# Graph layer in fp32 on one core: s added to x from PSUM tile by tile, three relus of four on ScalarE, no memsets on GpSimd, 104 early tiles instead of 96

## The chip, the cores and the metric

The kernel runs on one core of one Trainium2 chip. The metric is the device time of one execution in microseconds. Times shown as "runs" are medians of repeated executions; the profile is one further execution. The engines are named as in the profile: PE (TensorE) with PEld for its weight loads, DVE (VectorE), ACT (ScalarE), POOL (GpSimd) and SP (SyncE, which issues transfers only).

## The reference: what is computed

There are 12500 nodes with 160 features each (64 scalars and 32 vectors of 3) and 400000 edges, sorted by their target. Cut to what matters here:

```python
h = jnp.maximum(_layernorm(x, axis=-1), 0.0)       # no weight, no bias
s = [h0 @ W_sc0, h1 @ W_sc1] * a                   # per node, a = node_vec1
y = [h0 @ W_l1_0, h1 @ W_l1_1] * a                 # per node
w = silu(edge_attr_16 @ fc_W1) @ fc_W2             # per edge, 192 wide
mid = products of w, y[src] and edge_attr_4        # per edge, 96 scalars and 96 vectors
z = zeros.at[dst].add(mid)                         # sums over the edges of a node
out = x + C_S * s + C_X * [z0 @ W_l2_0, z1 @ W_l2_1] * a
```

The constant scales are folded into the weights in the kernel.

## The kernel before, in words

**Node stage.** The 98 tiles of 128 nodes are worked in 49 steps of two tiles; four steps are a group of eight tiles. `acc` in SBUF holds all of x, and later the output. The steps run as a software pipeline written out by hand: for each q the loop calls the stages with their lags, so that `turn_rows` of step q - 2 stands beside `center` of step q. `center` (DVE) takes mean and variance of each tile (`bn_stats`, `bn_aggr`) and makes h, the relu of x minus the mean: for the first tile of the step on DVE, for the second on ACT (`center_second`, with the negated mean `less` as bias). The division by the deviation comes last, since relu lets a positive factor through: `scales` turns the root that ACT took once a group into `ra`, a over the deviation. `turn_rows` (PE) transposes h, `out_of_psum` (ACT) brings it to SBUF as hT, `map_rows` (PE) multiplies with both weights at once, so that a tile of PSUM, `po`, holds y and s side by side, 2 x 160. There are six such banks. `leave` (ACT) scales po by ra into `ys` (y and s, 320 wide), and after the group's last step ACT stores the y half to `y_d` in DRAM. `add_s` (DVE) then adds the s half of the whole group, 8 x 160, to `acc` in one instruction. There are two `ys` buffers.

**Early batches.** The 3125 edge tiles form 782 batches of four. GpSimd gathers what a batch needs by one indirect transfer for each tile: rows of `y_d` by the edges' sources. That can't begin before all of `y_d` is written. So that GpSimd isn't idle in the node stage, it gathers rows of x itself, by the same indices, for some batches that come up later: `gather_x` brings them to `xr`, `keep_x` stores them to a scratch tensor `xr_d` (with a column of zeros set by DVE), and in the edge stage `made_load` ... `made_leave` compute y from them in small pieces between the other batches (statistics, relu, transposes, products with the weights; the node's a by a one-hot product). `made_at` lists these batches: RB of them, RS apart, in a first part (17, every 24 batches) and in a second (7, every 42). `plan` spreads the pieces over the batches before. A call `gather_x(j)` covers two tiles; it waits for hT of step j - 8, so that the gathers keep in step with the node tiles.

**Edge stage.** For each batch: `load` (POOL, four gathers of y into one of 11 buffers; the load of batch b waits for the weights of batch b - 8), `hidden` and `weigh` (PE, ACT: the edge weights in PSUM), `lift_rows` (ACT, L530), `dots_of` and `products` (DVE), `sums` (PE, L690: one-hot selection times products, summed in PSUM over a group of tiles). A finished group is transposed and mapped by PE and added to `acc` by DVE (`accumulate`, L735). The order on PE, ACT, DVE and POOL is that of the program in this stage; in the node stage POOL's and SP's order is made by the scheduler.

Before the edge stage, DVE finds each group's first node from `dst_i` (`first_nodes`, `all_nodes`, `relate`).

Of the kernel before, what the change touches and what calls it, by code (L numbers as in the profile page):

```python
# [17 lines left out]
P = 128  # L18
# [17 lines left out]
WIDE = 3, 5  # L36
GN = 8
HN = 2
RB = 17, 7
RS = 24, 42  # L40
LO = D - P
EPS = 1e-5
C_S = math.sin(math.pi / 8.0)
# [4 lines left out]
def kernel(  # L48
# [286 lines left out]
    engines = {mybir.EngineType.PE, mybir.EngineType.Activation, mybir.EngineType.DVE}  # L335
    with (
        tc.tile_pool(name="nr", bufs=1) as nrp,
        tc.tile_pool(name="nrx", bufs=10) as nrx,
        tc.tile_pool(name="ny", bufs=2) as ny,
        tc.tile_pool(name="ns", bufs=3) as ns,  # L340
        tc.tile_pool(name="nh", bufs=4) as nh,
        tc.tile_pool(name="nd", bufs=3) as nd,
# [30 lines left out]
        def gather_x(j):  # L373

            r, h = divmod(j, 2)
            if h == 0:
                xrs[r] = nrx.tile([P, GT * D + 1], F32, name="xr")
                nc.gpsimd.memset(xrs[r][:, :GT * D], 0.0)
                nc.gpsimd.memset(xrs[r][:, :D], 0.0)
            for k in (2 * h, 2 * h + 1):  # L380
                c = made_at[r] * GT + k
                of = src_first[:, r, k:k + 1] if r < FIRST else src_sb[:, c:c + 1]
                ins = nc.gpsimd.indirect_dma_start(  # L383
                    out=xrs[r][:, k * D:(k + 1) * D], out_offset=None, in_=x,
                    in_offset=bass.IndirectOffsetOnAxis(ap=of, axis=0))
# [10 lines left out]
        def center(q):  # L396

            g, n, j, m = steps[q]
            xt = acc[:, g:g + n, :]
            if j == 0:  # L400
                mvs[g] = ns.tile([P, GN, 2], F32, name="mv")
            mv = mvs[g]
            h = nh.tile([P, HN, D], F32, name="h")
            for k in range(m):
                st = ns.tile([P, 6], F32, name="st")
                nc.vector.bn_stats(st, xt[:, j + k, :])
                nc.vector.bn_aggr(mv[:, j + k, :], st)
                if k == 0:
                    nc.vector.tensor_scalar(h[:, k, :], xt[:, j + k, :], mv[:, j + k, 0:1], 0.0, ALU.subtract, ALU.max)
                else:  # L410
                    less = ns.tile([P, 1], F32, name="less")
                    nc.vector.tensor_scalar(less, mv[:, j + k, 0:1], -1.0, None, ALU.mult)
                    lesses[q] = less
            hs[q] = h
            if j + m == n:
                ra = ns.tile([P, GN], F32, name="ra")
                nc.scalar.activation(ra[:, :n], mv[:, :n, 1], AF.Sqrt, bias=eps)
                ras[g] = ra

        def center_second(q):  # L420

            g, n, j, m = steps[q]
            if m > 1:
                nc.scalar.activation(hs[q][:, 1, :], acc[:, g + j + 1, :], AF.Relu, bias=lesses.pop(q))

        def scales(q):

# [29 lines left out]
        def leave(q):  # L457

            g, n, j, m = steps[q]
            if j == 0:  # L460
                yss[g] = ny.tile([P, GN, 2, D], F32, name="ys")
            ys, ra = yss[g], ras[g]
            for k, po in enumerate(poss.pop(q)):
                nc.scalar.activation(ys[:, j + k, :, :], po, AF.Copy, scale=ra[:, j + k:j + k + 1])
            if j + m == n:
                node_dma(g, n, lambda rows, t, p: nc.scalar.dma_start(by_tile(y_d[rows, :]), ys[:p, t, 0, :]))

        def add_s(q):

            g, n, j, m = steps[q]  # L470
            if j + m == n:
                nc.vector.tensor_add(acc[:, g:g + n, :], acc[:, g:g + n, :], yss[g][:, :n, 1, :])


        with tc.manual_schedule(engines=engines):
# [35 lines left out]
            while begun[0] < 2 * nr:  # L511
                gather_x(begun[0])
                begun[0] += 1
            while kept[0] in xrs:
                keep_x(kept[0])
                kept[0] += 1
            first_nodes()
            edge_weights()
# [42 lines left out]
    with (  # L561
# [486 lines left out]
```

## Time and profile before

| | before |
|---|---|
| runs | median 3971.47 us of 3 (3970.27 to 3972.49) |
| the profiled execution's own time | 3969.84 us |
| its span, first to last instruction | 3967.8 us |
| TensorE's granted clock, mean | 0.976 |
| busy: PE, DVE, ACT, POOL | 92%, 88%, 48%, 76% |
| first gather of y | 150.5 us |
| gathers of y, of x | 3029, 96 |

A row of a timeline is start, duration, engine, line, operation, output and inputs, shape, how many instructions, and in brackets the idle time before it and what ended it. A row of a group is line, engine, operation, shape and count, then busy us and mean ns of one, then idle us before them and what ended it. POOL isn't counted busy in the pause of 0.3 us after each gather, which is why an engine that never waits shows 76%.

### The profile page before, as it was taken

Reading aid. Unit: us, or ns where it says so; the run is one execution under the profiler, and the core shown is the slowest. Engines: PE = TensorE matmul, PEld = TensorE weight load, DVE = VectorE, ACT = ScalarE, POOL = GpSimd, SP = SyncE. Lnnn points to the kernel's source line nnn. Section 1 sums busy time; section 2 is a strip of 40 time slices with the busy share of each in tenths; the row PEclk is TensorE's granted clock in tenths of the full one; section 3 lists DMA queues with packets and bytes.
Section 4 is the critical chain, followed back from the end, with each engine's and each line's share of the span. In section 5 each row is a group of like instructions: output and inputs, shape, how many; then the busy total and the mean of one; then the engine's idle time right before and its main releaser. Section 6 shows DMA issues by size and latency. Waiting matters only on the chain. (4 is left out here: it accounts for less than half of the span.)

```text
span 3967.8 us, 49385 instructions
## 1 busy us (share of the span) xinstructions
PE 3639.7 (92%) x15821; PEld 2102.0 (53%) x15821; DVE 3476.1 (88%) x6732; ACT 1906.6 (48%) x5350; POOL 2997.6 (76%) x3180
## 2 busy tenths in 40 slices
PE   6689999999999999999999989999999899999998
PEld 5445555555555555555555545555555555555554
DVE  6788888998888989989899888888889898989887
ACT  5544444444444444444544444444444444444443
POOL 8777777777777777777777777777777777777775
PEclk9899999999999999999999999999999999999999
DMA  8432333333223332322333332323333232342223
GB/s 267 140 76 74 77 77 79 79 77 79 73 77 77 80 79 77 79 74 77 77 79 79 77 76 74 78 74 76 77 76 77 74 79 74 80 124 76 73 75 84
DMA packets 228574, 334.77 MB, mean 84 GB/s; under 512 B 55098, under 2 KB 171910, under 8 KB 228054
## 3 DMA queue, kind: packets, MB, share of 16 engines
q0 software_dynamic: 150000, 256.20, 26.2%
q1 hardware_dynamic: 64642, 67.02, 5.4%
q10 hardware_dynamic: 13668, 8.36, 0.7%
q8 instruction: 125, 2.05, 0.2%
q14 instruction: 139, 1.14, 0.1%
HBM read 307.49 MB, written 23.88 MB: 84 GB/s over the span
## 5 line engine op out<-in xcount | busy, mean ns | idle before, releaser
L599 POOL DMA_INDIRECT yg<-y_d,src_sb x3029 | 2873.3, 949 | 923.3 <-issue 909.3
L690 PE MATMUL pz<-pr,sel 128*128 128x384 f32 x6250 | 2281.3, 509 | 2.2 <-ACT za L708 2.1
L530 ACT ACTIVATE yge<-yg,raw 128x160 f32<-128x160 f32 x3029 | 1253.7, 426 | 1903.1 <-DMA yg<-y_d,src_sb 1894.5
L690 PEld LDWEIGHTS pz<-pr,sel 128*128 128x128 f32 x6250 | 1150.9, 194 | 831.4 <-issue 227.9
L635 PE MATMUL pw<-w,hT 64*128 64x192 f32 x6250 | 732.1, 353 | 247.9 <-DVE pr L546 235.5
L635 PEld LDWEIGHTS pw<-w,hT 64*128 64x128 f32 x6250 | 497.5, 188 | 639.1 <-DVE pr L546 432.2
L542 DVE TENSOR_TENSOR pr<-pr,pw 128x768 f32<-128x768 f32 (+1 forms) x782 | 745.0, 953 | 27.0
L535 DVE TENSOR_TENSOR tmp<-yg,pw 128x384 f32<-128x384 f32 (+1 forms) x758 | 415.0, 548 | 325.4 <-ACT pw L637 322.5
L537 DVE TENSOR_REDUCE yg<-tmp 128x128 f32<-128x384 f32 (+1 forms) x758 | 449.8, 593 | 27.2 <-ACT yge L530 1.1
L669 DVE TENSOR_TENSOR sel<-pw,drel 128x1536 f32<-128x1536 f32 (+1 forms) x261 | 455.1, 1744 | 0.0
L617 PE MATMUL px<-xe,w 32*128 32x512 f32 x782 | 439.0, 644 | 10.7 <-ACT os L722 4.2
L541 DVE TENSOR_TENSOR pr<-pw,yg 128x384 f32<-128x384 f32 (+1 forms) x758 | 419.7, 554 | 17.8
L546 DVE TENSOR_TENSOR pr<-pw,yge 128x384 f32<-128x384 f32 (+1 forms) x782 | 427.1, 546 | 0.0
L545 DVE TENSOR_TENSOR pr<-pw,yge 128x256 f32<-128x256 f32 (+1 forms) x782 | 325.2, 416 | 0.0
L622 ACT ACTIVATE hT<-px 128x512 f32<-128x512 f32 x391 | 227.1, 581 | 11.7 <-PE px L617 11.5
L617 PEld LDWEIGHTS px<-xe,w 32*128 32x128 f32 x782 | 114.5, 183 | 197.2 <-issue 78.9
L637 ACT ACTIVATE pw<-raw 128x12 f32<-128x12 f32 (+1 forms) x782 | 129.1, 165 | 79.1 <-PE pw L635 78.8
L717 PEld LDWEIGHTS px<-wc,za 128*128 128x128 f32 x720 | 98.1, 191 | 29.2 <-ACT za L708 0.9
L383 POOL DMA_INDIRECT xr<-in_x,src_sb x88 | 93.4, 1061 | 22.7 <-issue 18.1
L735 DVE SCALAR_TENSOR_TENSOR acc<-os,by,acc 128x160 f32 x240 | 92.4, 385 | 18.4 <-ACT os L722 1.4
L717 PE MATMUL px<-wc,za 128*128 128x96 f32 x720 | 96.6, 270 | 0.6 <-ACT za L708 0.6
L704 PEld LDWEIGHTS pz<-ident,zs 128*128 128x128 f32 x360 | 46.7, 141 | 38.1 <-issue 21.1
(128 smaller groups left out, 1567.9 us busy)
## 6 DMA issues: line engine op xcount, KB each, us to landing
yg<-y_d,src_sb POOLq DMA_INDIRECT x3029
xe<-in_e SPq DMA_DIRECT2D x196, 128.0 KB
xr_d<-xr SPq DMA_DIRECT2D x24, 320.5 KB
y_d<-ys ACTq DMA_DIRECT2D x12, 640.0 KB
xm<-xr_d SPq DMA_DIRECT2D x24, 320.0 KB
acc<-in_x SPq DMA_DIRECT2D x11, 640.0 KB
out<-acc SPq DMA_DIRECT2D x11, 640.0 KB
raw<-in_e SPq DMA_DIRECT2D x32, 192.0 KB
```

What stands on the lines that cost most here:

```text
L530: return [nc.scalar.activation(yge[:, k, :], yg[:, k, :], AF.Copy, scale=e4v[:, k, 0:1]).ins for k in range(n)]
L535: return [nc.vector.tensor_tensor(tmp[:, :n], y1, wt[:, :n, NW:NW + 3].unsqueeze(3).to_broadcast([P, n, 3, M1]), ALU.mult).ins, nc.vector. ...
L537: nc.vector.tensor_reduce(yg[:, :n, M0:96], tmp[:, :n].rearrange("p t c u -> p t u c"), AX.X, ALU.add).ins]
L541: return [nc.vector.tensor_mul(pr[:, :n, 0:96], wt[:, :n, 96:NW], yg[:, :n, 0:96]).ins, nc.vector.tensor_mul(pr[:, :n, 256:].rearrange("p ...
L542: nc.vector.tensor_mul(pr[:, :n, 256:].rearrange("p t (c u) -> p t c u", c=3), pr[:, :n, 0:M0].unsqueeze(2).to_broadcast([P, n, 3, M0]), w ...
L545: nc.vector.tensor_mul(pr[:, :n, 96:160], wt[:, :n, 0:M0], yge[:, :n, 0:M0]).ins,
L546: nc.vector.tensor_mul(pr[:, :n, 160:256].rearrange("p t (c u) -> p t c u", c=3), wt[:, :n, M0:96].unsqueeze(2).to_broadcast([P, n, 3, M1] ...
L599: ins = [nc.gpsimd.indirect_dma_start(out=yg[:, k, :], out_offset=None, in_=y_d, in_offset=bass.IndirectOffsetOnAxis(ap=src_sb[:, t:t + 1] ...
L617: nc.tensor.matmul(ph, w1[r, :], xe[r, :], start=True, stop=True)
L635: ins.append(nc.tensor.matmul(pw[:, k, 0:NW], hids[s][r, o:o + P], w2[r, :], start=True, stop=True).ins)
L669: ins = nc.vector.tensor_tensor(sels[u][:, 0:n, :].rearrange("p t (k c) -> p t k c", k=GT), for_each, drel[:, u * TG:u * TG + n].unsqueeze ...
L690: nc.tensor.matmul(z_ps[g], sels[t // TG][:, t % TG, :], pr[:, k, M0:], start=first, stop=last)
```

## The change

It does six things.

- `add_s` runs for each step with lag 5: for each tile one `scalar_tensor_tensor` that reads the s half of `po` from PSUM, multiplies by ra and adds to `acc`. The addition of 8 x 160 a group goes.
- `leave` evacuates only the y half, 160 wide, and `ys` is half as large, with three buffers instead of two.
- In odd steps both relus run on ACT, in even steps one as before: three of four. `less` has two columns.
- The two memsets of each `xr` on GpSimd go. Its buffers are 13 instead of 10.
- There are 9 early batches in the second part, 33 apart, instead of 7, 42 apart: 104 early tiles instead of 96. Their pieces are 6 batches apart with lag 2, as in the first part, instead of 12 with lag 6.
- `scales` has lag 2 instead of 1; the load of dst is issued at step 24 instead of at the start; the `keep_x` calls left after the loop follow `first_nodes` and `edge_weights`.

```diff
-RB = 17, 7
-RS = 24, 42
+RB = 17, 9
+RS = 24, 33
...
-        tc.tile_pool(name="nrx", bufs=10) as nrx,
-        tc.tile_pool(name="ny", bufs=2) as ny,
+        tc.tile_pool(name="nrx", bufs=13) as nrx,
+        tc.tile_pool(name="ny", bufs=3) as ny,
...
                 xrs[r] = nrx.tile([P, GT * D + 1], F32, name="xr")
-                nc.gpsimd.memset(xrs[r][:, :GT * D], 0.0)
-                nc.gpsimd.memset(xrs[r][:, :D], 0.0)
...
+            of = range(m) if q % 2 else range(1, m)
             for k in range(m):
...
-                if k == 0:
+                if k not in of:
                     nc.vector.tensor_scalar(h[:, k, :], xt[:, j + k, :], mv[:, j + k, 0:1], 0.0, ALU.subtract, ALU.max)
-                else:
-                    less = ns.tile([P, 1], F32, name="less")
-                    nc.vector.tensor_scalar(less, mv[:, j + k, 0:1], -1.0, None, ALU.mult)
-                    lesses[q] = less
+            if len(of):
+                less = ns.tile([P, HN], F32, name="less")
+                nc.vector.tensor_scalar(less[:, of[0]:m], mv[:, j + of[0]:j + m, 0], -1.0, None, ALU.mult)
+                lesses[q] = of, less
...
-            if m > 1:
-                nc.scalar.activation(hs[q][:, 1, :], acc[:, g + j + 1, :], AF.Relu, bias=lesses.pop(q))
+            if q in lesses:
+                of, less = lesses.pop(q)
+                for k in of:
+                    nc.scalar.activation(hs[q][:, k, :], acc[:, g + j + k, :], AF.Relu, bias=less[:, k:k + 1])
...
-                nc.scalar.activation(ys[:, j + k, :, :], po, AF.Copy, scale=ra[:, j + k:j + k + 1])
+                nc.scalar.activation(ys[:, j + k, :], po[:, 0, :], AF.Copy, scale=ra[:, j + k:j + k + 1])
...
-            if j + m == n:
-                nc.vector.tensor_add(acc[:, g:g + n, :], acc[:, g:g + n, :], yss[g][:, :n, 1, :])
+            for k, po in enumerate(poss[q]):
+                to = acc[:, g + j + k, :]
+                nc.vector.scalar_tensor_tensor(to, po[:, 1, :], ras[g][:, j + k:j + k + 1], to, op0=ALU.mult, op1=ALU.add)
...
-            nc.sync.dma_start(dst_i, dst)
...
+                if q == min(24, last):
+                    nc.sync.dma_start(dst_i, dst)
...
-                for stage, lag in ((scales, 1), (center_second, 1), (out_of_psum, 3), (leave, 6), (turn_rows, 2), (map_rows, 4),
-                                   (center, 0), (add_s, 7)):
+                for stage, lag in ((scales, 2), (center_second, 1), (out_of_psum, 3), (leave, 6), (turn_rows, 2), (map_rows, 4),
+                                   (center, 0), (add_s, 5)):
...
-            step, lag = (6, 2) if b * GT <= wide else (12, 6)
+            step, lag = 6, 2
```

What this makes of the instructions' order, at three places. On GpSimd, at the very start (x of the first batches; the numbers tell buffers apart, and a name in brackets is the semaphore's owner that is waited for: DMAHW for SP's and ACT's transfers, DMASW for GpSimd's own). Before:

```order
L378 MEMSET xr_194 128x640
L378 MEMSET xr_201 128x640
L379 MEMSET xr_194 128x160 [waits Pool_49]
L379 MEMSET xr_201 128x160 [waits Pool_49]
L378 MEMSET xr_208 128x640
L383 DMA xr_194<-in_x,src_first_141 128x160 [waits DMAHW0_49,Pool_49]
L383 DMA xr_194<-in_x,src_first_141 128x160 x3
```

And now, after the same memset of `wor`:

```order
L490 MEMSET wor_107 128x480
L381 DMA xr_193<-in_x,src_first_141 128x160 [waits DMAHW0_49]
L381 DMA xr_193<-in_x,src_first_141 128x160 x3
L381 DMA xr_198<-in_x,src_first_141 128x160 [waits DMAHW2_49]
L381 DMA xr_198<-in_x,src_first_141 128x160 x3
L381 DMA xr_203<-in_x,src_sb_69 128x160 [waits DMAHW6_49,DMASW0_49]
```

Of the memsets none is left; the first gather waits for the transfer of its indices alone.

On DVE, around the end of a group's statistics in the node stage. Before, two tiles of one step and the addition of the group two before:

```order
L406 BN_STATS st_462<-acc_111 128x6
L407 BN_AGGR mv_403<-st_462 128x2 [waits DVE_49]
L409 TENSOR_SCALAR h_461<-acc_111,mv_403 128x160 [waits DVE_49,PE_49]
L406 BN_STATS st_466<-acc_111 128x6
L407 BN_AGGR mv_403<-st_466 128x2 [waits DVE_49]
L412 TENSOR_SCALAR less_469<-mv_403 128x1 [waits DVE_49,Activation_49]
L472 TENSOR_TENSOR acc_111<-acc_111,ys_333 128x1280 [waits Activation_49]
```

And now, one odd step, without a relu on DVE:

```order
L405 BN_STATS st_485<-acc_111 128x6
L406 BN_AGGR mv_394<-st_485 128x2 [waits DVE_49]
L405 BN_STATS st_488<-acc_111 128x6
L406 BN_AGGR mv_394<-st_488 128x2 [waits DVE_49]
L411 TENSOR_SCALAR less_491<-mv_394 128x2 [waits DVE_49,Activation_49]
L474 SCALAR_TENSOR_TENSOR acc_111<-po0_135,ra_374,acc_111 128x160 [waits PE_49,Activation_49]
L474 SCALAR_TENSOR_TENSOR acc_111<-po1_136,ra_374,acc_111 128x160 [waits PE_49,Activation_49]
```

Every step now ends on DVE with two additions that wait for PE, and for ACT's earlier reading of the bank.

On ACT, the evacuations of one step and the store of a group. Before:

```order
L424 ACTIVATE h_640<-acc_111,less_648 128x160 [waits DMAHW1_49,DVE_49]
L445 ACTIVATE hT_656<-pt0_133 128x512 [waits PE_49,Activation_49]
L464 ACTIVATE ys_568<-po4_139,ra_500 128x320
L464 ACTIVATE ys_568<-po5_140,ra_500 128x320
L466 DMA y_d_60<-ys_568 128x8x160 [waits DMAHW7_49,Activation_49]
```

And now:

```order
L425 ACTIVATE h_637<-acc_111,less_645 128x160 [waits DMAHW1_49,DVE_49]
L446 ACTIVATE hT_655<-pt0_133 128x512 [waits PE_49,Activation_49]
L465 ACTIVATE ys_566<-po4_139,ra_493 128x160 [waits DVE_49]
L465 ACTIVATE ys_566<-po5_140,ra_493 128x160 [waits DVE_49]
L467 DMA y_d_60<-ys_566 128x8x160 [waits DMAHW3_49,Activation_49]
```

The evacuations now wait for DVE, which reads s from the same bank first; the store still waits for an earlier transfer on a semaphore that it shares with SP's.

More of the change, by code (lines that the diff above doesn't have):

```diff
@@ L460, in leave @@
             if j == 0:
-                yss[g] = ny.tile([P, GN, 2, D], F32, name="ys")
+                yss[g] = ny.tile([P, GN, D], F32, name="ys")
             ys, ra = yss[g], ras[g]
             for k, po in enumerate(poss.pop(q)):
-                nc.scalar.activation(ys[:, j + k, :, :], po, AF.Copy, scale=ra[:, j + k:j + k + 1])
+                nc.scalar.activation(ys[:, j + k, :], po[:, 0, :], AF.Copy, scale=ra[:, j + k:j + k + 1])
             if j + m == n:
-                node_dma(g, n, lambda rows, t, p: nc.scalar.dma_start(by_tile(y_d[rows, :]), ys[:p, t, 0, :]))
+                node_dma(g, n, lambda rows, t, p: nc.scalar.dma_start(by_tile(y_d[rows, :]), ys[:p, t, :]))
         def add_s(q):
             g, n, j, m = steps[q]
-            if j + m == n:
-                nc.vector.tensor_add(acc[:, g:g + n, :], acc[:, g:g + n, :], yss[g][:, :n, 1, :])
+            for k, po in enumerate(poss[q]):
+                to = acc[:, g + j + k, :]
+                nc.vector.scalar_tensor_tensor(to, po[:, 1, :], ras[g][:, j + k:j + k + 1], to, op0=ALU.mult, op1=ALU.add)
         with tc.manual_schedule(engines=engines):
@@ L513 @@
                 begun[0] += 1
+            first_nodes()
+            edge_weights()
             while kept[0] in xrs:
@@ L516 @@
                 kept[0] += 1
-            first_nodes()
-            edge_weights()
     before.close()
```

## The prediction

> **What bounds the kernel now.** I read the page first, then the waits of the whole span, then GpSimd's own timeline, because the shares alone mislead: TensorE is busy 92% and GpSimd only 76%.
>
> ```profile
> span 3967.8 us, 49385 instructions
> ## 1 busy us (share of the span) xinstructions
> PE 3639.7 (92%) x15821; PEld 2102.0 (53%) x15821; DVE 3476.1 (88%) x6732; ACT 1906.6 (48%) x5350; POOL 2997.6 (76%) x3180
> ```
>
> Among the groups on the page are the gathers of y, and those of x (busy us, mean ns of one, idle before):
>
> ```profile
> L599 POOL DMA_INDIRECT yg<-y_d,src_sb x3029 | 2873.3, 949 | 923.3 <-issue 909.3
> ```
>
> ```profile
> L383 POOL DMA_INDIRECT xr<-in_x,src_sb x88 | 93.4, 1061 | 22.7 <-issue 18.1
> ```
>
> The second view is the table of waits over the whole span (engine and line, what it waited for, total us, times, longest).
>
> ```profile
> ACT yge L530 <- DMA yg<-y_d,src_sb: 1894.5, 2209, 3.9
> POOL yg L599 <- issue: 909.3, 2983, 0.3
> ```
>
> The gathers of y wait for nothing but their own issue, never longer than 0.3 us, while ScalarE waits 2209 times for what they fetch. GpSimd is the bound of the whole edge stage, with idle time only between its own instructions. Its timeline gives the rate and the places of the start and the end:
>
> ```profile
> 3.79 1.09 POOL L383 DMA_INDIRECT xr<-in_x,src_first  x1 [0.17 <-POOL xr L378]
> ...
> 74.33 1.60 POOL L383 DMA_INDIRECT xr<-in_x,src_sb  x1 [0.30 <-issue]
> ...
> 149.23 0.97 POOL L383 DMA_INDIRECT xr<-in_x,src_sb  x1 [0.30 <-issue]
> 150.51 0.95 POOL L599 DMA_INDIRECT yg<-y_d,src_sb  x1 [0.30 <-issue]
> ...
> 3945.87 0.94 POOL L599 DMA_INDIRECT yg<-y_d,src_sb  x1 [0.30 <-issue]
> ```
>
> From the first gather of y to the last, the 3029th, are 3795.4 us, 3028 steps of 1.2534 us. After the last one 21.9 us remain to the end of the span; they are the last products and the stores, which the change doesn't touch. So the span is: when the first gather of y starts (150.5), plus 1.2534 us for each gather of y, plus 21.9 us. The change can act on the first two only.
>
> What sets 150.5? GpSimd came straight from its last gather of x (149.23). It wasn't waiting for y, which was ready earlier. ScalarE's timeline shows this:
>
> ```profile
> 18.48 0.58 ACT L445 ACTIVATE hT<-pt 128x512 f32<-128x512 f32 x1
> ...
> 131.03 0.61 ACT L445 ACTIVATE hT<-pt 128x512 f32<-128x512 f32 x1
> ...
> 139.51 1.28 ACT L622 ACT_TABLE_LOAD   x1 [3.90 <-DMA y_d<-ys]
> ```
>
> The first and last rows of hT are those of steps 0 and 48 of the node stage: 112.55 us for 48 steps, 2.345 us each. The table load waited for the last stores of y, so y was complete at 139.5, which is 8.5 us after the last hT and 11.0 us before GpSimd came for it. **In the node stage, too, GpSimd was last.**
>
> **The change, part by part.** Fewer gathers of y: 26 batches instead of 24 are made early, so 104 tiles of x are gathered instead of 96, and 3021 of y instead of 3029. In the edge stage that is 8 x 1.2534 = 10.0 us less. The 8 gathers of x go ahead of it, where they cost the same if GpSimd is last there, and nothing if it would wait for y anyway.
>
> GpSimd ahead of the first gather of y. Its 146.7 us from 3.79 to 150.51 hold 96 gathers (120.3 us at 1.2534), the memsets, and something else. These are groups of lines in the first 165 us, shapes apart:
>
> ```profile
> L472 DVE TENSOR_TENSOR acc<-acc,ys 128x1280 f32<-128x1280 f32 x12 | 17.8, 1487 | 4.6 <-ACT ys L464 4.6
> ...
> L378 POOL MEMSET xr<- 128x640 f32 x24 | 17.1, 725 | 0.0
> ...
> L379 POOL MEMSET xr<- 128x160 f32 x24 | 5.7, 244 | 0.4
> ```
>
> The memsets sum to 22.8 us. Five stand ahead of the first gather, at most 2.7 us by these means (3 x 0.725 + 2 x 0.244), and some lie within the pause that a gather has anyway. The rest of the 26.4 us is in the gathers themselves: those of x take 1061 ns, those of y 949, which makes 88 x 0.112 = 9.9 us, and the long ones stand under VectorE's large additions, as the 1.60 us at 74.33 does under the one at 73.63:
>
> ```profile
> 13.51 2.54 DVE L409 TENSOR_SCALAR h<-acc,mv 128x160 f32<-128x160 f32 x1
> ...
> 23.53 0.30 DVE L409 TENSOR_SCALAR h<-acc,mv 128x160 f32<-128x160 f32 x1
> 23.75 0.32 DVE L406 BATCH_NORM_STATS2 st<-acc 128x6 f32<-128x160 f32 x1
> ...
> 73.63 1.48 DVE L472 TENSOR_TENSOR acc<-acc,ys 128x1280 f32<-128x1280 f32 x1
> ...
> 3957.50 0.81 DVE L735 SCALAR_TENSOR_TENSOR acc<-os,by,acc 128x160 f32 x2 [0.83 <-ACT os L722]
> ```
>
> Both go: the memsets by the edit, the large additions because s now comes from PSUM tile by tile. For that form the nearest row is L735, which runs 240 times between gathers of 949 ns, so I take no hold-up from it. GpSimd would be through with x at 3.8 + 104 x 1.2534 = 134.2; at best 2.7 earlier (no memsets ahead of the first gather), and some 2 us later where VectorE's cast of dst falls on gathers as the additions did: 131.5 to 136.
>
> A rule of the Trainium skill speaks to this (SBUF — State Buffer, Who interferes with whom): an addition with both inputs in SBUF contends with GpSimd's reads only, and building descriptors needs the write interface, an inference by its own words. By that the additions hold up no gather and the 9.9 us would stay; the stretched gathers disagree, and I go by them (what would follow otherwise is the fourth rival).
>
> The node stage itself, which now may come last. VectorE per step of two tiles: the large addition goes (1.487 / 4 = 0.37 us), and so does half a relu, which held VectorE for 23.75 - 23.53 = 0.22 us (0.11 a step). Two additions from PSUM come. No row has that form at this size: at most it costs what L735 does, 0.81 us for two; at least what the relu does, 0.44. I take 0.75, near L735, which is the same operation. VectorE changes by -0.04 to +0.33 us a step, my value +0.27. ScalarE gains half a relu a step, 24 in all, and evacuates half the width 98 times; these are its groups in the same window:
>
> ```profile
> L464 ACT ACTIVATE ys<-po,ra 128x320 f32<-128x320 f32 x98 | 46.3, 535 | 5.2 <-DMA y_d<-ys 4.7 <-ACT ys L464 0.5
> ```
>
> ```profile
> L424 ACT ACTIVATE h<-acc,less 128x160 f32<-128x160 f32 x49 | 21.0, 429 | 30.9 <-DVE less L412 15.8 <-DVE mv L407 6.7 <-DVE st L406 3.9
> ```
>
> Half as wide, an evacuation costs between half of 535 and the 429 of a relu of that width; with 24 x 429 ns added that is -16 to 0 us, and 30.9 us of idle time before the relus is left. ScalarE doesn't set the pace.
>
> Waits that fall:
>
> ```profile
> DVE ra L431 <- ACT ra L417: 12.9, 9, 6.0
> ```
>
> ```profile
> ACT ys L464 <- DMA y_d<-ys: 4.7, 3, 3.0
> ```
>
> With the scales a step later (lag 2) VectorE no longer stands at the reciprocal right behind ScalarE's root, and with three y buffers ScalarE needn't wait for the store two groups back. Together they are 17.6 us, 0.37 a step. Not all goes: ScalarE's stores still wait in turn with SP's transfers, and VectorE now waits for TensorE's results at every step. I take 0.2 of it. The pace is then 2.345 + 0.27 - 0.2 = 2.4 us, between 1.95 and 2.68. Step 0 comes earlier by the relu at 13.51, which took 2.54 us under GpSimd's memsets instead of 0.30: 18.5 - 2.2 = 16.2. So y is complete at 16.2 + 48 x 2.4 + 8.5 = 139.9.
>
> **What is late next** is thus the node stage, not GpSimd: GpSimd would be free at 134 and wait some 6 us for y. Only here does it stop being the bound. The sum: the first gather of y starts at 139.9 instead of 150.5, -10.6; 8 gathers less, -10.0; together -20.6 us. The span goes to 3947, the profiled execution from 3969.84 to 3949 us. The median of the runs was 3971.47, 1.6 above that execution, so I forecast 3951 us.
>
> Edits that I cost at nothing. The pacing of the gathers of x (one pair 8 steps behind a step's hT): at 2.4 us a step it stays ahead of GpSimd's 2.5 us a pair; beyond 2.7 it would stall x, but then y is later still. The load of dst, moved on SP's queue behind the first stores of x to scratch: it is read after the last step, 24 steps of 2.4 or 58 us on. The last memsets and stores of kept x, moved behind the reductions over dst on VectorE: they wait for gathers that end by 136, and GpSimd doesn't wait for them. VectorE may enter the edge stage further behind GpSimd than now; eight batches, 32 x 1.2534 = 40 us, may lie between them before GpSimd must wait.
>
> Nine early batches stand 33 batches apart in the last two fifths, not seven 42 apart, with their steps at 6 instead of 12. Windows of 600 us in the first part, where there is one in 24 batches, and of 205 us in the last:
>
> ```profile
> 1600.00:2200.00 600.00, 565.46 (x2452) 323.82 (x2453) 541.25 (x1034) 294.71 (x830) 454.00 (x480) 0.99 0.30 77
> ...
> 3215.00:3420.00 205.00, 190.71 (x837) 111.05 (x835) 180.75 (x343) 98.19 (x288) 155.01 (x165) 0.98 0.30 76
> ```
>
> The columns are the width, then busy us of PE, PEld, DVE, ACT and POOL. The dense part runs with PE at 94.2% and DVE at 90.2%, and GpSimd still never waits. The thin part has 93.0% and 88.2%. One set more in 33 batches is no denser than that.
>
> **Rivals.** First, GpSimd stays last: additions from PSUM near the lower price, waits gone, a pace of 2.27 or less. Then y is there by 134, the first gather at 134, -16.5 - 10.0: 3945 us. For it: the lower bound of the pace is 1.95. Against: VectorE was the fullest engine and gets more work. Chance 0.27.
>
> Second, the other side: the node stage slows so much that it eats the gain. Mechanism: a tile of PSUM now has two readers that go one after the other, VectorE's addition and then ScalarE's evacuation, and behind both TensorE's next write. At a pace p y is complete at 24.7 + 48 p; the gain of 10.0 is gone at 160.5, p = 2.83, and the kernel is measurably slower from 168.5, p = 3.0; with p = 3.2 the time is 3971.5 + 27.8 - 10 = 3989 us. For it: the waits are in the new program, and VectorE has no slack. Against: the two work on steps one apart with six banks, and p = 3.2 needs 0.5 us a step beyond my upper bound. Chance 0.05. The Trainium skill has the rule for these waits (PSUM — Partial Sum Buffer, PSUM bank collisions raise a hardware error): two engines must not be in one bank at once, reads included; the row of L735 can't show what that costs.
>
> Third, the change doesn't gain what it says in the second part: the denser early batches put TensorE behind, GpSimd stalls on its buffers, and the 10.0 us come back; with the rest as forecast 3961 us. Against it are the windows above. Chance 0.08.
>
> Fourth, the gathers of x stay long: what stretches them is not the additions but something that the change leaves. Then x is done at 134.2 + 9.9 = 144.1, GpSimd is last after all, and the time is 4.2 above mine, 3955 us. For it: two rows side by side are no proof of a cause. Against: gathers of y, which meet no such additions, take 949 ns throughout. Chance 0.08. This is also the outcome by the page on SBUF in the Trainium skill.
>
> My forecast, the node stage last at 137 to 147, has 0.52: 3948 to 3958 us.
>
> **How the numbers follow.** The range takes in the first rival, mine and the fourth, 0.87 in all: 3942 (x done at 131.5) to 3959 leaves out rivals two and three. A measurement of this kernel can tell about 0.2%, 8 us, from no change: faster means below 3963.5. All but the second rival and a part of the third lie there: 0.93; within 0.2%: 0.04; slower: 0.03.
>
> **What would show it.** Right: no memsets between gathers of x, none of these over 1.2 us except at a cast, the first gather of y between 134 and 147 behind the last store of y, steps of 1.2534 us to the end, and 21.9 us behind the last. hT of step 48 near 131. Wrong: a first gather of y after 150 (the pace), gaps over 0.3 us among the gathers of y past 2600 us (the third rival), or long gathers of x that remain (then the additions weren't what stretched them).

## The result, and the profile after

The changed kernel takes 3945.12 us (median of 4 runs, 3936.48 to 3947.08), the kernel before 3970.89 us in the same set. The ratio is 0.9931, interval 0.9918 to 0.9943. In a later set it was 3934.05 us against 3959.74, ratio 0.9937 (0.9923 to 0.9951). The gain is 25.8 and 25.7 us; the prediction had 20 (3951 us), and the time that came out is that of its first rival: 3945 us, GpSimd last throughout. The profile below is of the quickest of the four, 3936.48 us; the other three took 3945.08 to 3947.08, so its span is not that of the median. All ratios leave out two executions that stood far apart: one of b_104_tiles, 5031 us at a granted clock of 0.653, and one of a_cast_act, 16843 us.

The page of the changed kernel, total span and engines, the two groups of gathers, and from the table of waits the two lines that carried the argument before:

```profile
span 3934.6 us, 49703 instructions
PE 3647.5 (93%) x15893; PEld 2114.9 (54%) x15893; DVE 3486.8 (89%) x6853; ACT 1911.5 (49%) x5404; POOL 2959.8 (75%) x3132
```

```profile
L602 POOL DMA_INDIRECT yg<-y_d,src_sb x3021 | 2859.0, 946 | 920.4 <-issue 908.8
...
L381 POOL DMA_INDIRECT xr<-in_x,src_sb x96 | 92.1, 960 | 30.9 <-issue 13.2
```

```profile
ACT yge L533 <- DMA yg<-y_d,src_sb: 1837.4, 2155, 3.9
POOL yg L602 <- issue: 908.8, 2983, 0.3
```

GpSimd still waits for nothing in the edge stage, and the gathers of x have come down from 1061 to 960 ns. Its timeline shows where the stage now begins and ends:

```profile
2.64 1.09 POOL L381 DMA_INDIRECT xr<-in_x,src_first  x1 [1.08 <-DMA src_first<-in_src]
...
124.52 2.31 POOL L381 DMA_INDIRECT xr<-in_x,src_sb  x1 [0.30 <-issue]
...
134.62 0.94 POOL L381 DMA_INDIRECT xr<-in_x,src_sb  x1 [0.30 <-issue]
135.87 0.94 POOL L602 DMA_INDIRECT yg<-y_d,src_sb  x1 [0.30 <-issue]
...
3913.99 0.95 POOL L602 DMA_INDIRECT yg<-y_d,src_sb  x1 [0.30 <-issue]
```

The first gather of y starts at 135.87 instead of 150.51, 0.30 us behind the last gather of x, which is the pause that every gather has. It did not wait for y. One gather of x alone is long, at 124.52, under VectorE's cast of dst. From the first to the last gather of y are 3020 steps of 1.2510 us, and 20.6 us remain behind the last.

The node stage is quicker than forecast. ScalarE's timeline has hT of steps 0 and 48, and VectorE's a pair of the new additions with the instruction behind it:

```profile
16.74 0.58 ACT L446 ACTIVATE hT<-pt 128x512 f32<-128x512 f32 x1
...
121.28 0.61 ACT L446 ACTIVATE hT<-pt 128x512 f32<-128x512 f32 x1
```

```profile
75.51 0.68 DVE L474 SCALAR_TENSOR_TENSOR acc<-po,ra,acc 128x160 f32<-128x160 f32 x2
76.10 0.32 DVE L405 BATCH_NORM_STATS2 st<-acc 128x6 f32<-128x160 f32 x1
```

That is 104.54 us for 48 steps, 2.178 us each (before 2.345, forecast 2.4). Two additions hold VectorE for 76.10 - 75.51 = 0.59 us. The groups of the first 165 us:

```profile
L474 DVE SCALAR_TENSOR_TENSOR acc<-po,ra,acc 128x160 f32<-128x160 f32 x98 | 33.5, 379 | 5.2 <-PE po L455 5.0
L425 ACT ACTIVATE h<-acc,less 128x160 f32<-128x160 f32 x73 | 28.8, 427 | 32.3 <-DVE less L411 17.4 <-DMA w<-in_fc_w 9.8 <-DVE acc L474 4.2
L432 DVE RECIPROCAL ra<-ra 128x8 f32<-128x8 f32 x12 | 2.3, 194 | 0.0
```

VectorE's wait for the root is gone (12.9 us before). Another has grown: ScalarE, at its relus, waits once for 9.8 us for a weight load of SP, which held it for 2.2 us before.

### The profile page after: what moved, and what is told of

Same layout as the page of the kernel before. It is cut to its first block, busy times and chain, and to the rows that moved or that the text cites. A ratio compares the mean times of both kernels' runs of the same rounds, so it can differ in the third digit from the quotient of the medians.

```text
span 3934.6 us, 49703 instructions
## 1 busy us (share of the span) xinstructions
PE 3647.5 (93%) x15893; PEld 2114.9 (54%) x15893; DVE 3486.8 (89%) x6853; ACT 1911.5 (49%) x5404; POOL 2959.8 (75%) x3132
## 5 line engine op out<-in xcount | busy, mean ns | idle before, releaser
L538 DVE TENSOR_TENSOR tmp<-yg,pw 128x384 f32<-128x384 f32 x756 | 414.5, 548 | 295.7 <-ACT pw L640 292.2
L540 DVE TENSOR_REDUCE yg<-tmp 128x128 f32<-128x384 f32 x756 | 448.5, 593 | 26.8 <-ACT yge L533 0.7
L544 DVE TENSOR_TENSOR pr<-pw,yg 128x384 f32<-128x384 f32 x756 | 418.8, 554 | 17.8
```

Of the source, the lines that this page charges most:

```text
L538: return [nc.vector.tensor_tensor(tmp[:, :n], y1, wt[:, :n, NW:NW + 3].unsqueeze(3).to_broadcast([P, n, 3, M1]), ALU.mult).ins, nc.vector. ...
L540: nc.vector.tensor_reduce(yg[:, :n, M0:96], tmp[:, :n].rearrange("p t c u -> p t u c"), AX.X, ALU.add).ins]
L544: return [nc.vector.tensor_mul(pr[:, :n, 0:96], wt[:, :n, 96:NW], yg[:, :n, 0:96]).ins, nc.vector.tensor_mul(pr[:, :n, 256:].rearrange("p ...
```

## Experiments

Names that begin with b are made from the kernel before, names with a from the changed one. Differences in microseconds are between medians of the same set, unless it is said otherwise; the place of the first gather of y, which is what the experiments move, comes from the profile.

**The memsets alone.**

```diff
-                nc.gpsimd.memset(xrs[r][:, :GT * D], 0.0)
-                nc.gpsimd.memset(xrs[r][:, :D], 0.0)
```

> The kernel before without the two memsets of each buffer of x; nothing else changes. Theory (GpSimd's own work ahead of the first gather of y sets the time, until y is late): gathers of x from 2.6 us on, 96 x 1.2534 + 9.9 us of stretch, so x is done at 132.8; y was complete at 139.5 and comes 2.2 us sooner, since the relu of step 0 no longer lies under memsets: first gather of y at 137.3, 13 us less, 3958 us. Rival A (the memsets lie in pauses that the gathers have anyway): 3971, no change. Rival B (y isn't late, the whole 22.8 us of busy time come back): 3948 us.

Measured: 3950.49 against 3959.77 us, 9.3 us less (forecast 13), ratio 0.9976 (0.9967 to 0.9985). GpSimd's group of gathers of x, the end of x on its timeline, and ScalarE's table load:

```profile
L381 POOL DMA_INDIRECT xr<-in_x,src_sb x88 | 93.4, 1061 | 26.8 <-issue 14.3 <-DMA xr<-in_x,src_sb 4.9 <-ACT ys L462 3.4
```

```profile
130.68 2.07 POOL L381 DMA_INDIRECT xr<-in_x,src_sb  x1 [0.30 <-ACT ys L462]
138.00 0.94 POOL L597 DMA_INDIRECT yg<-y_d,src_sb  x1 [5.26 <-DMA xr_d<-xr]
```

```profile
137.23 1.28 ACT L620 ACT_TABLE_LOAD   x1 [5.36 <-DMA y_d<-ys]
```

x is done at 132.75 (forecast 132.8), and GpSimd waits 5.26 us, to just behind the last store of y at 137.2: y cuts the gain, as expected. The row itself names a store of kept x as what ended the wait; I read it as y's, because the trace's last packet of the stores of y ends at 136.3, 1.7 us before, and in the three variants below whose rows name y it is 1.3 to 1.6 us. The gathers stay at 1061 ns, so it wasn't the memsets that stretched them.

**The additions from PSUM alone**: `add_s` and `leave` as in the changed kernel; all else as before.

```diff
-                nc.vector.tensor_add(acc[:, g:g + n, :], acc[:, g:g + n, :], yss[g][:, :n, 1, :])
+                nc.vector.scalar_tensor_tensor(to, po[:, 1, :], ras[g][:, j + k:j + k + 1], to, op0=ALU.mult, op1=ALU.add)
```

> The kernel before with s added tile by tile from PSUM and the evacuation half as wide; memsets, relus, lags of the scales, two y buffers and 96 tiles stay. Theory (the large additions stretch the gathers of x): these go from 1061 to about 950 ns, x is done 9.9 us sooner, first gather of y at 140.6, 3961 us, as long as y is there. Rival A (the rule of the Trainium skill, SBUF - State Buffer, Who interferes with whom, which would have such an addition hold up GpSimd's reads only): the gathers stay at 1061 ns and the time at 3971. Rival B (my term for the pace: 0.75 us of additions a step against 0.37 before, with none of the waits gone, 2.73 us a step): y complete at 158, 3979 us.

Measured: 3952.00 us, 7.8 us less (forecast 10), ratio 0.9981 (0.9972 to 0.9990). Groups, and the end of x:

```profile
L383 POOL DMA_INDIRECT xr<-in_x,src_sb x88 | 84.7, 963 | 23.4 <-issue 15.6 <-ACT ys L464 3.2 <-ACT h L424 2.0
...
L431 DVE RECIPROCAL ra<-ra 128x8 f32<-128x8 f32 x12 | 2.4, 197 | 2.0 <-ACT ra L417 2.0
```

```profile
139.59 0.95 POOL L383 DMA_INDIRECT xr<-in_x,src_sb  x1 [0.30 <-issue]
140.84 0.95 POOL L600 DMA_INDIRECT yg<-y_d,src_sb  x1 [0.30 <-issue]
```

The gathers fall to 963 ns and the first gather of y comes at 140.84 (forecast 140.6): the large additions had stretched them, and rival A falls. Rival B falls as well. hT runs from 18.47 to 127.81, 2.278 us a step; with two additions for a quarter of the large one the pace didn't rise to 2.73, it fell by 0.07. VectorE's wait for ScalarE's root went from 12.9 to 2.0 us although the scales still have lag 1.

**104 tiles alone.**

```diff
-RB = 17, 7
-RS = 24, 42
+RB = 17, 9
+RS = 24, 33
-        tc.tile_pool(name="nrx", bufs=10) as nrx,
+        tc.tile_pool(name="nrx", bufs=11) as nrx,
-            step, lag = (6, 2) if b * GT <= wide else (12, 6)
+            step, lag = 6, 2
```

> The kernel before with 104 early tiles instead of 96 (17 + 9, the second part 33 apart, steps of 6, 11 buffers of x); all else stays. Theory (GpSimd is last ahead of the edge stage as well as in it, so a gather that is moved costs there what it saves here): 8 gathers of y less, -10.0; 8 of x more, +10.0, with 4 more memsets (2 of 725, 2 of 244 ns), +1.9, and at most 1 us of stretch: 3971 to 3974 us, first gather of y at 162 to 163. Rival (each early tile is a gain of 1.2534 us of its own): 3961 us.

Measured: 3961.27 us, ratio 1.0006 (0.9997 to 1.0015). The first and the last gather of y:

```profile
160.07 0.95 POOL L599 DMA_INDIRECT yg<-y_d,src_sb  x1 [0.30 <-issue]
...
3938.16 0.95 POOL L599 DMA_INDIRECT yg<-y_d,src_sb  x1 [0.30 <-issue]
```

The first gather of y comes at 160.07 (forecast 162 to 163), 9.6 us later than before: the 10 us saved in the edge stage are spent ahead of it. An early tile is worth something only while GpSimd would otherwise wait for y.

**The changed kernel with 96 tiles.**

```diff
-RB = 17, 9
-RS = 24, 33
+RB = 17, 7
+RS = 24, 42
```

> The changed kernel with 96 early tiles (17 + 7, 24 and 42 apart; steps of 6 in both parts). Theory (in the changed kernel y is complete at about 129 us, 7 us before GpSimd comes): x is done at 135.6 - 10.0 = 125.6, GpSimd now waits for y until 129 to 130; 6 us won there, 10.0 lost by 8 more gathers of y: 4 us more than the changed kernel, 3949 us, and the first gather of y behind the last store of y. Rival A (y is ready sooner than I read it, or the gathers set its time): no change, 3945. Rival B (the two parts add up as in my prediction, y complete at 139.9): first gather of y later than 135.6, 3955 us.

Measured: 3941.39 us, ratio 0.9954 (0.9942 to 0.9967), some 7 us above the changed kernel by the two medians of different sets; forecast 4. The first gather of y, with what it waited for:

```profile
130.66 0.97 POOL L602 DMA_INDIRECT yg<-y_d,src_sb  x1 [8.02 <-DMA y_d<-ys]
```

Here GpSimd is ahead and waits 8.02 us. y is complete at 130.6, 9.9 us after hT of step 48 (120.78). In the variants below it takes 11.5 and 12.4 us. In the changed kernel, whose last hT is at 121.28, the last packet of the stores of y ends at 130.4; with the 1.3 to 1.6 us that follow it where GpSimd waits, y is there at about 132, some 4 us before GpSimd comes at 135.87. The eight tiles are worth 5 to 7 us here (10.0 less the 3.8 to 5.2 by which the first gather of y comes sooner without them; 7 by the medians) because of the other edits, not by themselves.

**The changed kernel again**, and three with one edit undone: the memsets back (a_memsets), the lag and the buffer (a_lag1_ny2), the third relu (a_one_relu).

```diff
+                nc.gpsimd.memset(xrs[r][:, :GT * D], 0.0)
+                nc.gpsimd.memset(xrs[r][:, :D], 0.0)
```

```diff
-        tc.tile_pool(name="ny", bufs=3) as ny,
+        tc.tile_pool(name="ny", bufs=2) as ny,
-                for stage, lag in ((scales, 2), ...
+                for stage, lag in ((scales, 1), ...
```

```diff
-            of = range(m) if q % 2 else range(1, m)
+            of = range(1, m)
```

> The changed kernel unaltered, beside the others of this set. Theory (span = first gather of y + 1.251 us for each further gather + the tail, the rate being that of the chip and not of the kernel): first gather of y within 1 us of 135.9 and the same 3020 steps; whatever the rate is here, the kernel before has it too, so the ratio is that of 25 us in 3965, 0.9935. Rival (the rate of 1.2510 us instead of 1.2534 is something that the change brought): the kernel before stays at 1.2534 on every chip and the ratio is 0.991.

> The changed kernel with the two memsets of each buffer of x back. Theory (a pair costs GpSimd its 0.9 us of busy time less some 0.2 that lie in the pause of a gather: from the kernel before with additions from PSUM, whose 96 tiles and 24 pairs took 16 us more than 96 gathers and the cast): 26 pairs, first gather of y at 152 to 154, 17 us more than the changed kernel, 0.4%. Rival A (y, there at 129, or the pace under the memsets sets the place): more than 154. Rival B (they lie beside other work): no change.

> The changed kernel with the scales at lag 1 and two y buffers again. By the term of my prediction (these waits are 0.2 us a step) hT of step 48 comes 9.6 us later, at 131, y is complete at 139 and the time 3 us more than the changed kernel. Theory now (the short evacuations have already taken most of these waits: in the kernel before with additions from PSUM the root held VectorE 2.0 us in all and the stores ScalarE 4.6): hT of step 48 at 121 to 126, y complete before 134, first gather of y still straight behind the last of x at 135.9, and no change.

> The changed kernel with one relu of two on ScalarE in every step, as before. Theory (VectorE sets the pace of the node stage, 2.05 us a step in stretches without a stall): half a relu more, 0.11 us a step, hT of step 48 at 126.5, y complete at 134.5, and no change of the time, since GpSimd comes at 135.9. Rival A (ScalarE sets the pace, with its chain from relu to transpose): hT of step 48 at 121 or sooner, no change either. Rival B (VectorE loses more than 0.14 us a step, so that y is last again): first gather of y behind the last store of y, 1 to 5 us more.

| | median, us | ratio to before | first gather of y, and what it waited for | last hT |
|---|---|---|---|---|
| a_same | 3934.05 | 0.9937 (0.9923 to 0.9951) | 134.44, its own pause | 121.09 |
| a_memsets | 3951.49 | 0.9980 (0.9971 to 0.9989) | 152.01, its own pause | 119.18 |
| a_lag1_ny2 | 3940.19 | 0.9951 (0.9937 to 0.9964) | 140.48, y for 6.75 us | 128.09 |
| a_one_relu | 3939.52 | 0.9951 (0.9937 to 0.9964) | 138.41, y for 4.17 us | 126.88 |

These are GpSimd's rows of the four, in the table's order (of a_same the first and the last gather of y), and the two groups of a_lag1_ny2 that waited:

```profile
134.44 0.94 POOL L602 DMA_INDIRECT yg<-y_d,src_sb  x1 [0.30 <-issue]
...
3911.82 0.95 POOL L602 DMA_INDIRECT yg<-y_d,src_sb  x1 [0.30 <-issue]
```

```profile
152.01 0.94 POOL L604 DMA_INDIRECT yg<-y_d,src_sb  x1 [0.30 <-issue]
```

```profile
140.48 0.94 POOL L602 DMA_INDIRECT yg<-y_d,src_sb  x1 [6.75 <-DMA y_d<-ys]
```

```profile
138.41 0.94 POOL L602 DMA_INDIRECT yg<-y_d,src_sb  x1 [4.17 <-DMA y_d<-ys]
```

```profile
L465 ACT ACTIVATE ys<-po,ra 128x160 f32<-128x160 f32 x98 | 33.0, 399 | 13.7 <-DMA y_d<-ys 13.7
...
L432 DVE RECIPROCAL ra<-ra 128x8 f32<-128x8 f32 x12 | 2.4, 199 | 16.4 <-ACT ra L416 16.4
```

a_same: the theory holds, though the first gather of y comes 1.4 us sooner where 1 was allowed. The rate is 1.2508 us here, and the kernel before is as much quicker in this set (3959.74 instead of 3970.89), so the ratio hardly moves. a_memsets: 17.4 us, as forecast; the 26 pairs of memsets cost 17.6 us of place, 0.68 us each instead of the 0.90 for which they are busy. a_lag1_ny2: my theory was wrong, and the term of the prediction came nearer. hT of step 48 is 7.0 us later, 0.146 us a step (the term said 0.2), VectorE stands 16.4 us at the root and ScalarE 13.7 at stores of y, and y is last. a_one_relu: hT 5.8 us later, 0.12 us a step (0.11 forecast), but I had put y at 134.5 by counting 8 us from the last hT; it needs 11.5, and GpSimd waits 4.17 us for it: rival B, 5.5 us more.

**The last set**, again from the changed kernel: 120 tiles (a_120_tiles), the cast of dst on ScalarE (a_cast_act), s added tile by tile from SBUF (a_sbuf_tiles, with `leave` of 320 columns as before, `add_s` at lag 7, two y buffers and 11 of x), gathers of half a row (a_half_rows, which leaves out the other half of what a gather brings and so doesn't compute the layer).

```diff
-RB = 17, 9
-RS = 24, 33
+RB = 17, 13
+RS = 24, 24
```

```diff
-        nc.vector.tensor_copy(drel, dst_i)
+        nc.scalar.activation(drel, dst_i, AF.Copy)
```

```diff
-                nc.vector.scalar_tensor_tensor(to, po[:, 1, :], ras[g][:, j + k:j + k + 1], to, op0=ALU.mult, op1=ALU.add)
+                nc.vector.tensor_add(to, to, yss[g][:, j + k, 1, :])
```

```diff
+        y_half = y_d.rearrange("n (h c) -> (n h) c", h=2)
-                out=yg[:, k, :], out_offset=None, in_=y_d,
+                out=yg[:, k, 0:D // 2], out_offset=None, in_=y_half,
```

> The changed kernel with 120 early tiles (17 + 13, one batch in 24 made early throughout). Theory (a gather moved ahead of the edge stage costs there what it saves in it, as the kernel before with 104 tiles showed): 16 gathers more ahead of the first of y, which starts at 134.4 + 20.0 = 154.5, 16 fewer behind it: no change, within 2 us of the changed kernel. Rival (the third of my prediction: denser early batches put the other engines behind, and GpSimd stalls on its buffers): gaps over 0.3 us between gathers of y past 2600 us, 5 to 20 us more.

> The changed kernel with the cast of dst to float on ScalarE instead of VectorE. Theory (the cast blocks GpSimd for its whole length: gathers under it took 2.12 to 2.31 us instead of 0.95): no gather of x over 1.2 us any more, first gather of y at 133.1 instead of 134.4 to 135.9, 1.3 us less, which is under what the times can tell; y, complete at 130 to 131, isn't in the way. Rival (the cast on ScalarE takes so much longer that VectorE's reductions behind it delay the first batch): no change or up to 2 us more.

> The changed kernel with s evacuated to SBUF again (320 wide, two y buffers of that width, 11 buffers of x) and added tile by tile, 128x160 with both inputs in SBUF. Theory (a gather is held only if its first moment, the reading of its indices, falls into such an addition, and then until the addition's end): with 98 additions of about 0.25 us in 115 us a fifth of the gathers waits 0.13 us, 2.6 us in all: mean of the gathers of x 0.98 to 0.99 us with the cast, none but that at the cast over 1.3 us. Rival A (the additions hold GpSimd in proportion to their total time, 25 us against 18 for the large ones): 10 us or more of stretch, mean 1.06 us. Rival B (only the large form does it): 0.960 us as in the changed kernel.

> The changed kernel with gathers of y that fetch 80 elements of a row instead of 160 (the first half of other rows; the other half of a buffer stays zero), to see what a gather's 0.95 us depends on. Theory (GpSimd's work is the 128 rows, not their bytes): 1.25 us a step as before, time within 10 us of the changed kernel. Rival (the bytes count): about 0.8 us a step, GpSimd no longer the bound, and TensorE (3644 us busy) next: 3750 to 3850 us.

In the executions compared here TensorE was granted a mean clock of only 0.886 to 0.898, and the kernel before took 4710.44 us. Times: 4694.01 (ratio 0.9975, 0.9953 to 0.9996), 4710.36 (1.0000, 0.9978 to 1.0023), 4714.72 and 4697.51 us, the last two single runs. The first lines are of a_cast_act: the clock in 40 slices, a window that was shown of the kernel before (columns as there, then clock, DMA share and GB/s), and GpSimd's waits:

```profile
PEclk8788889989898898898998888898998989899888
```

```profile
1600.00:2200.00 600.00, 520.43 (x2066) 290.70 (x2063) 453.12 (x861) 218.13 (x685) 385.74 (x408) 0.91 0.24 66
```

```profile
POOL yg L602 <- issue: 827.8, 2710, 0.8
POOL yg L602 <- remote: 419.2, 174, 4.8
POOL yg L602 <- PE pw L638: 360.5, 122, 9.9
POOL yg L602 <- DMA y_d<-ys: 18.0, 1, 18.0
```

In 600 us GpSimd issues 408 gathers instead of 480. It now waits 360 us for TensorE's weights, and 419 us for something that the trace doesn't name: it is not the bound here. The changed kernel, its cast aside, then equals the kernel before. The 0.25% of a_120_tiles goes with a granted clock of 0.896 in the middle, against 0.891 for a_cast_act and for the kernel before, so it can't be put down to the tiles. What 120 tiles and the cast do where GpSimd is the bound stays open; the cast fell behind the last gather of x here, so that nothing met it.

Two answers stand in the traces all the same. The groups of a_half_rows (gathers of y, and below them the DMA queue of GpSimd) and of a_sbuf_tiles (gathers of x, additions):

```profile
L606 POOL DMA_INDIRECT yg<-y_d,src_sb x3021 | 2852.6, 944 | 1631.0 <-issue 762.3
```

```profile
q0 software_dynamic: 101664, 132.46, 13.0%
```

```profile
L381 POOL DMA_INDIRECT xr<-in_x,src_sb x96 | 91.2, 950 | 55.7 <-ACT hT L446 29.8 <-issue 23.2 <-DVE st L405 1.2
...
L474 DVE TENSOR_TENSOR acc<-acc,ys 128x160 f32<-128x160 f32 x98 | 29.7, 322 | 24.2 <-ACT ys L465 18.2 <-issue 1.6 <-ACT hT L446 1.5
```

Half the bytes (132 MB on the queue, against 256 for a_cast_act) leave a gather at 944 ns, against 946 there: between these two sizes its price doesn't depend on the bytes. And additions with both inputs in SBUF hardly stretch the gathers when they are short: 950 ns on average, against 946 in a_cast_act. Ten gathers began inside such an addition, and all ten ended 0.81 to 0.82 us after its end, six of them lengthened by that to 0.97 us or more, at most 1.01. So the short form holds a gather too, only briefly: rivals A and B fall. The 0.98 to 0.99 that I had worked out was too much (it held the cast, which met no gather here).

## Why the prediction was right or wrong

**The bound and the form of the sum: right.** In the nine profiles of the changed kernel and the variants taken at a clock of 0.973 to 0.976 the span is the place of the first gather of y, 1.2507 to 1.2511 us for each further one, and a tail of 19.8 to 21.9 us. Against the kernel before, whose place is known from its own profile alone, place and count give each difference above to within 3.2 us; the worst is b_no_memsets, 12.5 by its place and 9.3 by the medians. What makes the rest isn't shown.

**Eight gathers fewer, -10.0 us: right as a term**, with its condition: b_104_tiles shows that it is spent ahead of the edge stage unless room is made there.

**GpSimd ahead of the first gather of y: right.** Of the 26.4 us that 96 gathers left unexplained, the prediction gave 9.9 to the large additions and the rest to the memsets. Undone one by one: the additions 150.51 - 140.84 = 9.7 us, the memsets 17.6 for 26 pairs. x was forecast done at 134.2, with 2 us more if the cast meets a gather; it was done at 135.56 (134.62 + 0.94), and at 134.14 in a_same.

**The pace of the node stage: the step that failed.** "The pace is then 2.345 + 0.27 - 0.2 = 2.4 us" was 2.18, so y was there at about 132 instead of 139.9, and GpSimd stayed last; that is the first rival, which had 0.27 against 0.52. The time lies within 3942 to 3959 because that range took in this rival; the forecast itself, 3948 to 3958 with y last, did not come. The mis-sized term is VectorE's own work. Its busy time (the third figure behind the width) from hT of step 0 to hT of step 48, before and after:

```profile
18.48:131.03 112.55, 87.70 (x566) 76.01 (x567) 85.96 (x342) 82.94 (x199) 93.42 (x107) 0.94 0.81 244
```

```profile
16.74:121.28 104.54, 84.88 (x565) 76.52 (x565) 87.60 (x401) 78.86 (x222) 77.86 (x83) 0.93 0.94 279
```

The work rose by 1.6 us, 0.03 a step instead of 0.27. The idle time fell from 26.6 to 16.9 us, by the 0.20 a step that the prediction took. Of the 0.24, 0.16 is the price of the two additions (0.75 taken by the row of L735, whose two instructions don't overlap; 0.59 here). Another 0.06 is the half relu: with it back on VectorE (a_one_relu) this engine is busy 94.40 us in the same stretch, against 86.37 in a_same, 0.17 a step for the 0.11 taken. In the pace the half relu is worth 0.12, since VectorE then waits less.

**The waits: the right sum, in part by luck.** The root's 12.9 us and the stores' 4.7 are gone altogether, 0.37 a step. Of what came in their place on VectorE, the 5.0 us at TensorE's results were foreseen, the 4.3 behind ScalarE's relus (L411) were not. The new lag and the third buffer are worth 0.146 a step (a_lag1_ny2), but b_adds_psum, which has neither, had lost 10.9 of the 12.9 us at the root already. The wait at the root is thus no property of the lag alone: with evacuations of half the width and one relu of two on ScalarE it is 2.0 us, with the third relu there 16.4, with the lag nothing. That ScalarE's load decides it is how I read these three; it wasn't tried by itself. Half of the 16.4 comes at once:

```profile
59.00 0.68 ACT L465 ACTIVATE ys<-po,ra 128x160 f32<-128x160 f32 x2 [9.20 <-DMA y_d<-ys]
```

```profile
61.28 0.20 DVE L432 RECIPROCAL ra<-ra 128x8 f32<-128x8 f32 x1 [8.43 <-ACT ra L416]
```

In a_lag1_ny2 ScalarE stands 9.20 us at a store of y, and VectorE 8.43 us at the root right behind it. The changed kernel's wait of 9.8 us for SP's weight load, which ends at 64.64, isn't there in a_lag1_ny2, and in b_adds_psum it is 2.6 us. So one wait of ScalarE takes another's place, and the parts don't simply add up: 2.278 of b_adds_psum less 0.12 and 0.146 is 2.01, where 2.18 came. What decides on whom that wait falls stays open.

**"What is late next": nearly.** It was said that the node stage would be. It isn't, but it is only some 4 us ahead of GpSimd: without the third relu, or without the lag and the buffer, GpSimd waits 4.17 and 6.75 us for y. Edits that look as if they did nothing in the changed kernel's own profile hold its gain.

**The second rival** (two readers of a bank of PSUM slow the stage beyond the gain) did not come: VectorE waits 5.0 us in all for TensorE's results (L474).

**The third** (denser early batches stall GpSimd): its waits in the edge stage are the 0.3 us pauses, up to the last gather at 3913.99. Refuted for 33 batches apart; for 24 apart it wasn't settled.

**The fourth, and the rule of the Trainium skill: I had read the rule too narrowly.** The gathers did get short, so the outcome that the prediction drew from the page didn't come. But the runs agree with the rule itself and show where the inference goes astray. VectorE's and GpSimd's timelines in b_no_memsets:

```profile
82.26 1.48 DVE L470 TENSOR_TENSOR acc<-acc,ys 128x1280 f32<-128x1280 f32 x1
```

```profile
81.88 0.95 POOL L381 DMA_INDIRECT xr<-in_x,src_sb  x1 [0.30 <-DMA xr<-in_x,src_sb]
83.13 1.43 POOL L381 DMA_INDIRECT xr<-in_x,src_sb  x1 [0.30 <-issue]
```

The gather that began 0.38 us before the addition took its usual 0.95 us under it. The one that began inside ended 0.82 us after the addition's end (84.56 against 83.74). In the three kernels with large additions 35 of the 36 gathers that began inside one were held, and all of these ended 0.81 to 0.83 us after its end; the 36th began 0.02 us in. None that began earlier was lengthened. So an addition holds a gather's first moment, not the 0.82 us that follow. That the first moment is the reading of the indices from SBUF is my inference; it is what the Trainium skill (SBUF — State Buffer, Who interferes with whom) would have, which says that an instruction of VectorE with two SBUF inputs contends with GpSimd's reads. With the second input in PSUM 27 gathers of a_same began inside an addition and took 0.94 or 0.95 us each. Short additions cost little by the same mechanism, since there is little time to wait. The cast is another thing. In b_adds_psum:

```profile
131.12 1.79 DVE L168 CAST drel<-dst_i 128x3136 f32<-128x3136 int32 x1
```

```profile
130.82 2.21 POOL L383 DMA_INDIRECT xr<-in_x,src_sb  x1 [0.15 <-issue]
```

This gather had begun 0.30 us before the cast and ended 0.12 us after it (133.03 against 132.91). The same section names casts among the instructions that can take both shared ports and block GpSimd wholly; the trace agrees in that a gather already begun is held too. It also works the other way: two gathers that had begun 0.65 and 0.67 us before a cast (a_memsets, a_lag1_ny2) took their usual 0.94 to 0.95 us, and there the cast lasted 1.92 and 1.90 us instead of 1.79.

## What to carry to other kernels

Where one queue issues at a fixed price, write the time as its start, its count times its step, and a tail, and ask of every edit which of the three it moves: a part that only shifts work along that queue (the eight tiles) is worth nothing until another part makes room. Price a pair of instructions by how long it keeps the next one from starting (0.59 us here), not by the row of another pair whose instructions don't overlap (0.81). When two engines are both near to being last, cost the wait that a shorter instruction upstream takes away as well as the one that a lag takes away, and keep the edits that give the runner-up its few microseconds. A long VectorE instruction with both inputs in SBUF beside GpSimd's gathers can hold one for most of its own length (up to 1.29 us for an addition of 1.48); the same additions from PSUM, or in short pieces, cost nearly nothing.

## What the hardware showed beyond that

The gathers' step differs between executions by 0.2%, whatever the kernel: 1.2534 us in the profile before, 1.2507 to 1.2511 us in nine later ones, made from either kernel. That is 7 us of a span, more than some of the edits here bring, and about what parts the profiled 3936.48 us from the other three executions of its set, of which there is no trace. So times are best compared within a set.

With a granted clock of 0.89 instead of 0.975, 9% less, the kernel before took 4710 us instead of 3960, 19% more, and the change was worth nothing there, as far as a_cast_act shows it (ratio 1.0000, 0.9978 to 1.0023). The gain in GpSimd's gathers was there only while TensorE was granted its clock. Why 9% of clock goes with 19% of time isn't shown.
